# Two expert rankings, unscaled token rows and a folded tail in a four-layer routed kernel

## The chip, the cores and the metric

The kernel runs on one core of one Trainium2 chip. The metric is the device time of one execution in microseconds. TensorE (PE in the profile), VectorE (DVE), ScalarE (ACT), GpSimd (POOL) and SyncE (SP) each run an instruction stream of their own and meet only at semaphores; SP issues most DMAs, POOL the indirect ones.

## The reference

The input is 16 sequences of 256 tokens of width 128, in float32. Four residual layers follow one another, each on the layer norm of its input. Cut to what is computed:

```python
# 1: "attention": softmax over the keys is contracted away from v, so it sums to one
att = softmax(einsum('blhd,bmhd->blmh', q, k) * scale, axis=2)
opt = einsum('blmh,blhd->blhd', att, v).reshape(b, l, d)
x = x + opt @ w_out.T + b_out            # i.e. (v @ w_out.T + b_out)
# 2 and 4: mixture of 8 experts, the best 2 for each token
gate_logits = xn @ gate_w
top_vals, top_idx = top_k(gate_logits, 2)
top_w = softmax(top_vals)
h = relu(einsum('td,edf->etf', xn, w1))          # d 128, f 512
x = x + einsum('etd,te->td', einsum('etf,efd->etd', h, w2), combine)
# 3: selective scan over the 256 steps, 16 states
delta = softplus((u @ W_x[:, :64]) @ W_dt + b_dt)
x = x + (scan(u, delta, A, B, C) + u * D) @ W_out + b_out
```

The two expert layers have the same weights `gate_w`, `w1` and `w2`.

## The kernel before

The 4096 tokens are worked in 8 blocks of 512 (`TB`). A block stays in on-chip memory as `x` (128 tokens in the partitions, 4 chunks, 128 wide). The attention layer is a matrix product with weights multiplied together beforehand (`wat`), and gives the logits of the first expert layer as well. The two expert layers are `k = 1` and `k = 2` in the code; from here on "layer 1" and "layer 2" mean these two. Each works through sets of blocks: `FIRST = ([0], [1], [2, 3], [4, 5], [6, 7])` and `SECOND = ([0, 1], [2, 3], [4, 5], [6], [7])`.

For each set, `route` chooses two experts for each token, counts tokens with products of 0/1 matrices (`both`, `before`, `onesb`), and so gives each token a place among an expert's slots. `choose` computes the shares of the two experts. For set [0] of layer 1 the rows go to their slots by products with 0/1 matrices (`spot`, `dealt`: `ramp` is compared with the place). For all other sets each row of 128 values is scaled and shifted by the share and the layer norm (`row`, on ACT or DVE) and scattered by GpSimd into a table in device memory (`slots`, `scatter` at L880, one indirect DMA for 128 tokens). `experts` then fetches the slots of one expert after another (`xs`), transposes them (`xsT`), multiplies with `w1` (into `ps_b` or `ps_B`), takes the relu (`h`), multiplies with `w2` (into `ps_y`), transposes back (`yT`, `yr`) and stores the result (`ys`). `collect` gathers each token's two rows (`yy`, L892, eight indirect DMAs for a block) and adds them to `x`. Since the share is positive, scaling the row ahead of the relu is the same as scaling the result.

A slot table is a list of (rows, columns) for each expert: `SLOTS` gives 8 slots of, say, 108 x 3 = 324. In layer 2 the experts are ranked once by their token counts (`ranking`, `RANKED = (2,)`), so that the largest slot goes to the fullest expert, and the weights are loaded again in that order: `load_experts` reads each rank's expert number from `which` into a register of SP (L934) and issues the loads of `w1` and `w2` (L935, L940). If a count exceeds a slot (`beyond`), the whole computation is done again by a general path at the end.

After each layer-1 set, `arrive` collects, takes the layer norm (`statistics`, `rstd_of`) and runs `mixer`, the selective scan of the set's blocks: logarithms and exponentials on ACT, scans and products on DVE, products with 0/1 selections on PE (`pieces`, `sel`). Its end multiplies the scan's result with `W_out`, and the input `u` with `wsd_s` = D times `W_out`. After each layer-2 set, `finish` collects, transposes and stores the result (`out_T`).

Nothing is issued as it is written down. Every operation becomes a job of a planner (`plan.job`, all recorded at L772), some with several engines to choose from (`either`). The planner starts jobs in the order of a list of ranks found beforehand (`ORDER`, packed text) and its own costs, and writes out each engine's program from the result. Where it foresees PE idle for 0.5 us or more, it inserts products of a block of zeros (`blank`, L1705), one for every 0.26 us. Buffers (`xT`, `row`, `yy`, `u`, `th` and others) have fixed numbers of copies.

Of the kernel before, what the change touches and what calls it, by code (L numbers as in the profile page):

```python
# [11 lines left out]
BF16 = mybir.dt.bfloat16  # L12
# [7 lines left out]
P = 128  # L20
L = 256
# [11 lines left out]
    {  # L33
        "first": ((88, 2),) * 8,
        1: ((84, 2),) * 8,
        2: ((108, 3),) * 8,
    },
    {
        "first": ((126, 3), (112, 3), (108, 3), (98, 3), (96, 3), (88, 3), (126, 2), (117, 2)),
        1: ((98, 2), (91, 2), (88, 2), (80, 2), (84, 2), (75, 2), (70, 2), (128, 1)),  # L40
        2: ((126, 3), (117, 3), (110, 3), (104, 3), (108, 3), (96, 3), (90, 3), (126, 2)),
    },
)
RANKED = (2,)
UNIT = 2
JOIN = 2

COLD = 5.0
# [14 lines left out]
    "c-qZZ2V4_p|G(!F2uWCBZ^GVNMD}nMWhmmpRjsY4t)oufI_lQiswi$nt>RvFf>K)%!~%*UB1=HoJFEa1cmE`Jxw{}(`+wi}^LZ0U"  # L63
    "a?kVJZ+?H@-|v>G_^I*=>c6NNCEAl^pxer^W>rkfI9&R;>iv%8rd7`B9lu02joA1NUDGqgsne+5m*>sC|3s_)i)v%K>WE364%f`z"
    "G%9VWd>|BeK0IC08FfuyS$#TV!ssUsJvZ9pw@tBaV2TlOKM(^Ype&9CWvPXsXYyKG+Pu%zXlZI1Sm&A}IY4CALbDer*&iR4gwV&l"
    "%_}jzc_s5zX!X3PvIWf#4x)X!&c}M*s#~aW*_FM4<>R>>-Ss7LRsE&oXUE3!i@n2)%YK;$2Ux%Q=KJd&AzO97EXmqll<=(G$|n86"
    "dYcDRExkEyN=&Uj^@^>Aca=O|2u`0WZ*KkZPp*nx>bjin<VsZC<o=9uRhFUFl+z=MPhNm~zw4pXzFM^_s$-IHUykn8ElEaxc^26-"
    "@4I$-U9_@v4^`W~w0Z1KeP?YmwJLUVr{|Jk*2t*vvi=>escnr%S2%5T@YvyUd1cK_&1T~j6D^|8^}R6ZVc4@5r`2UVu#9lkK^d>j"
    "<5raWMYj1fEzYZOy26KDMUnzv7Ki#3$Js3MGeWdkH_RQX!$+g^SGwX*L0g)m*&ht^hr`B{m+-Z+MtiQ=%kQlyO?ID9`_|x>g>x4a"
    "7{0aWT9KvwE7Mny<Gx<_BC^rwXq|G-%~+*L?XOC-N_X*TlWs>d*t>6dr4MgmZ>V5Cdl#UwvuaJIa7A;6SkO9NyAy2)R#I*_c4irG"  # L70
    "f$}i1aA)c7s#VilXwygk=1!Yh4K5@zA4WBp!hdS2*QXZDe|&PBD<YV-*P?Y!iDl#0qE3S>ix*QK?M<<E=x(XAp(VMh1?XG@R;LUe"
    "^+r5mvX*|O{~BSeh+)#r_1}t5_Zhr&a6Vyi`WybF4oh}yO!N4+5htCOsU-6w+usb|b1Ki@BBPCK;{T?1ty+gYBRIVexWd-=;yaSJ"
    "&s)c$pQk1Mu(kK>{gXydj2^f9i*!A>vkJ$Aory7?vCXs9d*QbqY<=vPD_5viZHRw+xyi_Maei$clW%G}<<Bhkhz`r&MH-;Cg^e&a"
    "U3gYoEtvixd0S^(bWqX_ezZ?DQW4gCxKZW)U-sXiwFV<^9XWugj&I$OH!^<jINSI_Rp(0X8CAy1J2}<+XY8MsQOzx+FI`ck!)UF1"
# [12 lines left out]
    "W}lxb*X~)HAE-1pB;BQ^LG!O|{!7wateXuPjy1g47G;AAOE#v|-`IO4l;JX=Le)SmG4aUQQQ6kXA%1z9t<NK0dmq^jAGBJpuKxgd"
    "eXkawFZ5$JMr2mlKB{8c=h)_Zy$KD=PPGs%xvk#g-~MD_9aH;}d%czM@ozmdc5X7%n7k(1V&fu#xkh5jB_tPq;C45@tIXzkaGgr;"
    "`U-V}elJ1K5|2t9!%F4Ie79N)zMgFdqAF5lr;az799pBdl=r?p=s{9t<;`CXoASO{t7VrlBRG@0J_1I0K8Wt`_lI$swmu6BI^+PG"
    "R<t`R#ilQeDPFoWaTfD_W-45&V`fle={DiT+;e$tuyA_JGv2os@98-1FqqaFKEJbL>3+MFs}kA@zjoxM2@bBZ-Zv|~*-qnO412%B"  # L90
    "Hrl?39I;U2Nl)*kc{(>WG8$)ax|gm~8_)17zHBvazRBVuOO~Pjb<fxgT5}Y$rBU13yY<|T>gT@6y{t2fvzNc1KieD~H?c3yIG5%1"
    "EZC;L<sGZu9pMPV16%ccCfxd9<XECrYvkB!<h1ocr=`%<`N@intL=VX)*h7_ooi=p!&4c>U}btmTfv<omWIQ-a$8N>Cfiq*;mz*K"
    "X~Rn9R^2?n+niWz_x`eL{ozpO&1-+YWLh^$VDQqHpSVriI0n@^F|pk#E1}=9&or)NWV*op*e;vXrU5-JJxh-3Fk{-vL_ZWd-(`H2"
    "k@>2&TjXi*rq>P$e>>}7fV!t%UxR&U@8s&d;UV$g>F5|2Zpc2S=4zO^Jm5y+3zK*Htk~qyL5(?+wC+!_Zq6Cy`MkJ=^V`TyeWuXt"
    "&YapiOGBTs*#<0g<ztSzO#Mb4*Oi?TS!SZ4o^E#ZOhD4zQ=R+|Ixbw%HSS}*_Wf~Z>nrHuK4p{B+fH~UE>nKqtaR_P_PR4V=)GIP"
    "!Ikr-C#gjoJ>T&4m`N)*+szxBUi?zstQE)^-*auA<Lrx}7Gn-|ZG9f9D$<H~iw)(J4uc)c&AfL9uaDPpx~_b%G&X4U1Ad5jy|0kt"
    "-q%m7eTec@?E3E4PPX$n(aU-rFg1Mb6W;3N3jQ<IiG33%{1O-0xc2P#Mc2LUH4C!)1d=i2$+S8jbn2MmrUfI44!n=6D`;&|bw8)y"
    "MfYYF)pRR$)vNK;YU^v8rn%{zpSh*DMQ>#O<%u3}gHdkWyZcHxnY}jZ*J4i7EpLtfqkWEhOIbWuuiJ~hV{K6Q^&if?00DY0hVOmz"
    "w(r2s*FMAf{wuvbzY9&%5hrHsZXcB!Frs-!vd?v~)$Q@#yhiOE3(d+F)HQFI-@S##Q8iU@>%DG>IK7Hv8*S0w$rzhkaXC6o)ji8s"
    "`!Bs^j7RVnPN~uUeqGnob@xW?s`toU?B})Hci%{(+x}N#%V$Pprx$y2*!ij>)2t(qr7We8OpgM4w#&%LI@|8^R%NLE{xFwj+K}6m"  # L100
    "b#UGJVz!Frr07J=%-<$(E^!5ZPiC$>cICE-+9D&MvC_q=&c?IIp#PomyfstNq`8xn_PPi{-i^Qb^B4icKWSfnWuEpshKGMXO-KBa"
    "=BoRm!22z7$df~xYih~RD4J0_uHf#=@y4}b4=0M=y}F&4Z()!27mYJDP#W|4r2qBc5k6+ZsmEp;lr-B_g}@On;%JxdtZy7=+QdGx"
    "yla*QO+TGe7qCPrt6tNs!1LsF+YX1c?FNBPU%_hnsIm6g1-Z(n%9a$4aLcXI(=D#wS?k^4&KOZ*`&&}y{2h1Nf(s*Ou)a7J-V;=5"
    "`P4q4-{LJlR5<M0=6>%|UzTqL+sN`e7sJ_KZg8@&@au7ONDB*z{gWFQUT1pQv}Vx+x9Hik#V7Rl+Z)hgxUIJA$4R$lKR?^2v3_#!"
    ">)PnR%R2jnzwLTu3Uu|kbtp<>T=OyQvM-&@w&$T@l}_3ZQ*NSLbH51^?E9;{t@f*o)tW*1N!vbj^|Lw3#=Yep4jt^mESpJxfC&!u"
    "_j<e<oHm85F<l%mC!pg^x#5;03HD#!nfc|W!Yv&~&3er&Hy#Y)c(sHwV#d^Ud=anS!QbqV|0JrT#@hFbW6e=28?RYgY;T}n^*esh"
    "+f#V-iGLybGSv_*tJ;;?#RTx?(>iSLS`GI|w-ybT=8a5-_S(Yg$bBX;2j0eVis|qA3g-E?KhJwV&Eu78T5)&z_y-)N`nxw$=*&I4"
    "nhaG+6Gw5t#PeFdh8BM?nN!+Kv}|TAVpYGdJksWFbWPdEPrax`*`nI_smPJjoW9V~)4$rh{Hwd?rzM>5KH{xeU~?{qv)X@bwaNGe"
    ")x-IJX?GXCn)i~Eud^+i|FF}2fgg*J(jGL=RLf9Ds3%lLgmgZP3Rit!p{KueP0iNqr)s^1@ATAXG1~3xEHC=8+jSqsm<GQY-k>pQ"
    ")26Pj?OzImt0t%IsMxt?=i!-Gh6e~9#%wsV?(#{Io<pJE>XcJn%Ns6MP24iQF89_rCD#Uf-P`BFQ~M6Jc2~515XG41nN2a6)1;bE"  # L110
    "m9@~*SLdZJ(|1(cZ01i#E9Vq@<!E+PUq1frrHS4?A+2}9m|xC1VIK0-!PJeR+T5nr?um*uelVfaw1czLr>d(b&f%Z*r3db5o>pvD"
    "`NQjpr{~RJ>@8@V<dHV^YS9#ylOs6LK3xClqaeM6-{Nw4$gz<rc6I;iujBWg&9<GqpiZA&YIlNb<X8M){?VWfCRNMIbh&NiE1&N1"
    "Z)j9s@Gvl`Y>8Xtz7RCT=GVN5u`IzgtLDSyJ$X|nn{9KuYVNy<-8-VKtT=$@bYzTU#`UzY*>5iKJ9gj9*!RX?q?ymqFZ`{jH=#dF"
    "LMgBGR>#`RU)1{GUJx_TxW`#X6lteYa@u-UM?{JPr%!4B&Uj^?lyyz|di?iqoTuHYJHFy^@6W$RU;VLQX5R=0?W@+@lIqBsIAigQ"
    "Lod6vLU(*~aevVHb7lFXY*M;Z+Wy7P8RO4teqXL1baF~l;@4^Gy48K7qFi-Wq+Lk(v!+AUC%4M)+MJagRk=b$>!C|sL46-2d7&r@"
    "N#BU%r}R?#DY-%+WdQ<7_W-_(;(PcvgdId>OEMv{f5~ZpP}U&qn>;Vyk*^VQrB?uvE0BExF(v`C60;V<h06_x#Q-}(SOXDiAqWAO"
    "9t7V8*xiz4L?(|^0O1NC=_ZPj#zOd8Vvgi?>>L7PTYz*yeh9w<m28P&6v5&Li-{nRj#K=Wg&eaDk;WbZ0QZDADR&JL(l8l77D!Y?"
    "NAb8(WXevF@qoyPqY|qS5uL~+L}rNyvpi$cILWqvKyHiF8!S)=;i>EdN~RK5i-#WjM+k4QyJf<qP?2VtP)Ec=43nP7v?BNcdA!9i"
    "Ay}qI?hA~_)+Oh$$YFLtG!f|-EXJ~fJ1n~oA<F>Zctc1}@N)<}0Q#605Y=-CONJCE2&RMz4IBX2Zv>Uelct-fKnO<|0ScKsF{uKD"
    "U<|SdL_s~7X$1cvko^L<ZXhdYIXD4IDP7qT20f|oR7Su~hyel<<sl0m>8j*5sWmiduBAo-nh*jI!3oke2u5-KkmVX7s!RdhKujqk"  # L120
    "dDbCH3W!paMhSr+62An-3BjZS5e!jiMj}q6jNpYYtq*zB5itx=M9DxeF$l)xU_d5`2e(oL<EaD)iB;kNW-eZqhzxLeZ2K65<<fuY"
    "r6Mw9-?C*YM#*Y`Aju|4j2M6cW+_4tk|b3q?kh<-eKL2k6d?eY4)DCngd=!ip@0MoHCytE#JraJCriA{Ln$9(?gBC%5TsDtq}h;S"
    "_E0%a@Km9IC@48aQ9FSg8Hjuf_f%d5&`0!#P@^cvJ_5+nl@T^dFflY}^^z?TC8=L54Iv=mOzA|BtVCddP-t9YA3y+E=h!BtxrzZ{"
# [1652 lines left out]
```

## Time and profile before

| | us |
|---|---|
| median of 3 runs (lowest to highest) | 471.61 (468.14 to 472.38) |
| the profiled execution | 467.84 |
| its span, first to last instruction | 466.1 |
| PE busy, 2670 records | 447.0 |
| of these, products of `blank`, 232 records | 31.2 |
| DVE busy | 345.6 |
| POOL busy | 311.8 |
| ACT busy | 268.3 |
| data moved by DMA | 55.37 MB, mean 119 GB/s |

The span is what the profile divides into stages; the time of an execution is 1.7 us longer than the span here. A group in the profile is named by its line, engine, operation and the tiles that it writes and reads. Nearly all groups have line 772, because all operations are recorded there, so the tile names tell them apart.

### The profile page before, as it was taken

What the parts mean: (1) busy time and instruction counts of PE and PEld (TensorE: products, weight loads), DVE (VectorE), ACT (ScalarE), POOL (GpSimd) and SP (SyncE); (2) the same over time, 40 slices, a digit from 0 to 9 for tenths busy, and PEclk for the clock granted to TensorE, in tenths of its full rate; (3) what the DMA queues carried; (4) which work ended last, traced back from release to release, by engine and by line L of the source; (5) the groups of instructions that cost most, each with busy time, mean ns of one, the idle gap of its engine ahead of it and who ended that gap; (6) DMA issues with size and microseconds to landing.
All of it is one profiled execution on the core that took longest, in us unless ns stands there. A gap on an engine that the chain in (4) does not pass through costs nothing.

```text
span 466.1 us, 8797 instructions
## 1 busy us (share of the span) xinstructions
PE 447.0 (96%) x2670; PEld 355.8 (76%) x2670; DVE 345.6 (74%) x1229; ACT 268.3 (58%) x621; POOL 311.8 (67%) x482
## 2 busy tenths in 40 slices
PE   8999999999999999989997999989999999999994
PEld 6889998866766667665665777677678877999993
DVE  4799999778697878999999998996786931223420
ACT  2124443577576854995889496797735534343310
POOL 8188787777673761276866776836785477778662
PEclk9999999999999999999999899999999999999999
DMA  5974234632352423236644322144225333543251
GB/s 155 340 244 135 71 122 134 166 107 66 108 155 67 114 78 96 65 106 195 188 121 142 93 73 76 53 120 132 69 58 146 114 113 90 135 125 91 78 164 45
DMA packets 74917, 55.37 MB, mean 119 GB/s; under 512 B 8184, under 2 KB 66800, under 8 KB 74864
## 3 DMA queue, kind: packets, MB, share of 16 engines
q1 hardware_dynamic: 66640, 38.35, 28.5%
q0 software_dynamic: 7936, 16.27, 12.1%
q8 instruction: 23, 0.38, 0.4%
q14 instruction: 30, 0.25, 0.2%
q10 hardware_dynamic: 288, 0.13, 0.1%
HBM read 28.95 MB, written 25.77 MB: 117 GB/s over the span
## 4 chain that ended last, share of the span: by engine, by line
PE 72%; DVE 16%; ACT 4%; issue 3%; POOL 2%; DMA 1%; POOLq 0%; DVEq 0%; ACTq 0%
PE ps_b L772 25%; PE ps_y L772 24%; PE ps_B L772 21%; DVE x L772 3%; DVE ps_B L772 2%; DVE stats L772 2%; PE ps_y L1705 2%; POOL yy L892 2%; DVE w L772 1%; DMA yy<-ys,of 1%; DVE th L772 1%; ACT th L772 1%; DVE rt L772 1%; ACT decay L772 1%; DVE u L772 1%
## 5 line engine op out<-in xcount | busy, mean ns | idle before, releaser
L892 POOL DMA_INDIRECT yy<-ys,of x128 | 125.5, 980 | 64.4 <-issue 37.2
L880 POOL DMA_INDIRECT slots<-row,to x120 | 120.6, 1005 | 49.5 <-issue 19.4
L772 PE MATMUL ps_y<-h,w_s 128*128 128x324 f32 (+13 forms) x552 | 145.2, 382 | 0.0
L772 PE MATMUL ps_B<-xsT,w_s 128*128 128x324 f32 (+9 forms) x352 | 112.8, 442 | 0.8 <-DVE w L772 0.4
L772 PEld LDWEIGHTS ps_y<-h,w_s 128*128 128x128 f32 x552 | 90.4, 190 | 20.3 <-issue 1.3
L772 PEld LDWEIGHTS ps_B<-xsT,w_s 128*128 128x128 f32 x352 | 61.7, 191 | 23.8 <-issue 3.2
L772 ACT ACTIVATE h<-ps_B 128x648 f32<-128x648 f32 (+9 forms) x62 | 43.8, 707 | 33.5 <-PE ps_B L772 33.1
L772 PE MATMUL ps_b<-xsT,w_s 128*128 128x176 f32 (+9 forms) x288 | 54.8, 316 | 1.2 <-ACT yr L772 1.2
L772 PEld LDWEIGHTS ps_b<-xsT,w_s 128*128 128x128 f32 x288 | 44.1, 190 | 2.7 <-ACT yr L772 1.5
L772 ACT COPY yT<-ps_y 128x324 f32<-128x324 f32 (+14 forms) x52 | 18.8, 362 | 36.0 <-PE ps_y L772 35.2
L772 ACT ACTIVATE th<-later,lneps,ha_s 128x112 f32<-128x112 f32 (+13 forms) x85 | 39.1, 507 | 0.2 <-DVE th L772 0.2
L772 ACT ACTIVATE h<-ps_b 128x352 f32<-128x352 f32 (+9 forms) x47 | 22.3, 474 | 26.0 <-PE ps_b L772 24.1
L772 PE MATMUL ps_b<-ident,yT 128*108 128x128 f32 (+11 forms) x177 | 34.4, 274 | 0.7 <-ACT yr L772 0.7
L772 ACT COPY xsT<-ps_b 128x324 f32<-128x324 f32 (+15 forms) x52 | 19.1, 372 | 26.6 <-PE ps_b L772 25.3
L772 ACT ACTIVATE decay<-delta,nea 128x108 f32<-128x108 f32 (+13 forms) x85 | 31.7, 412 | 2.7 <-DVE delta L772 2.6
L1705 PE MATMUL ps_y<-blank,ones_d 128*128 128x128 f32 x232 | 31.2, 293 | 1.3 <-DVE blank L772 1.3
L772 DVE TENSOR_TENSOR_SCAN w<-decay,ps_B 128x360 f32<-128x360 f32 (+7 forms) x40 | 31.0, 802 | 1.3 <-ACT decay L772 0.5
L1705 PEld LDWEIGHTS ps_y<-blank,ones_d 128*128 128x128 f32 x232 | 30.0, 208 | 1.6 <-DVE blank L772 1.3
L772 ACT COPY yr<-ps_b 108x384 f32<-108x384 f32 (+13 forms) x50 | 21.3, 425 | 16.8 <-PE ps_b L772 16.8
L772 ACT ACTIVATE row<-x,mp,rp 128x128 f32<-128x128 f32 x63 | 28.1, 488 | 3.6 <-DVE rp L772 2.0
L772 PE MATMUL ps_b<-ident,xs 108*128 108x108 f32 (+13 forms) x186 | 29.7, 256 | 0.1
L772 DVE TENSOR_SCALAR h<-ps_B 128x648 f32<-128x648 f32 (+6 forms) x26 | 21.3, 819 | 11.1 <-PE ps_B L772 10.8
(207 smaller groups left out, 792.2 us busy)
## 6 DMA issues: line engine op xcount, KB each, us to landing
w_s<-in_w SPq DMA_DIRECT2D x32, 256.0 KB
xs<-slots SPq DMA_DIRECT2D x27, 162.0 KB
ys<-yr SPq DMA_DIRECT2D x27, 162.0 KB
slots<-blank SPq DMA_DIRECT2D x2, 1280.0 KB
xT<-in_xT SPq DMA_DIRECT2D x8, 256.0 KB
yy<-ys,of POOLq DMA_INDIRECT x128
out_T<-xnT SPq DMA_DIRECT2D x8, 256.0 KB
slots<-row,to POOLq DMA_INDIRECT x120
```

The lines of the kernel that those rows point to most:

```text
L772: return lambda: f(*[real(x) for x in a], **{n: real(x) for n, x in k.items()})
L880: inst = nc.gpsimd.indirect_dma_start(out=real(out), out_offset=bass.IndirectOffsetOnAxis(ap=real(rows), axis=0), in_=real(in_), in_offset ...
L892: nc.gpsimd.indirect_dma_start(out=real(out), out_offset=None, in_=real(in_), in_offset=bass.IndirectOffsetOnAxis(ap=real(rows), axis=0),)
L1705: nc.tensor.matmul(out=spare, lhsT=ones_d.real(), rhs=blank.real(), start=True, stop=True,)
```

## The change

- `SLOTS` gives each set a table of its own, and layer 1 is ranked too, from set [2, 3] on: `RANKED = ((1, 2), (2, 0))`. The weights are therefore loaded three times instead of twice.
- Scatters send the unscaled rows of `x`. `w1` is centred when first loaded, by a product with `centre` (the identity less 1/128), so that the mean needs no subtraction; the share times the reciprocal deviation is applied in `collect`, with four `scalar_tensor_tensor` instructions for each gathered tile in place of one add.
- The centred `w1` and `w2` are written back to device memory (`w1c`, `w2c`) in the layout of on-chip memory, in runs of 2 KB; later loads come from there, with the eight expert numbers loaded into registers of SP at once (`look`).
- A set's slots lie one after another in the table, no longer interleaved by expert.
- `mixer` scales `u` by 2 D, adds the scan's result to it, and needs one product with `wsh_s` = half of `W_out`, where it had two.
- For the last set, [7] of layer 2, the results of the last three experts (`LATE = 3`) are not stored and gathered: `marks` builds each token's share at its slot as a matrix, and `finish` adds `yr` times the marks into the output's bank.
- In the dealing of set [0], the shares are left out of the 0/1 matrices, and ACT may build them too (`Away`: an absolute value and a relu). The reciprocal deviation of block 0 is started by a `pow` on POOL.
- `ORDER` is another list, and some costs of the planner differ. The number of inserted `blank` products follows from these.

```diff
-RANKED = (2,)
+RANKED = ((1, 2), (2, 0))
 UNIT = 2
+LATE = 3
...
-                idle[i] = (start[i] - free) * (1.0 if start[i] > COLD else 0.5)
+                idle[i] = start[i] - free
...
-    def load_experts(k):
+    w1c, w2c = dram("w1c", [NE, P, FF]), dram("w2c", [NE, P, FF])
+
+    def load_experts(q):
         for r in range(NE):
...
+                pw = bank("B", P, FF)
+                matmul(pw, centre, into[0])
+                copy(into[0], pw)
+                move(w1c[r], into[0], 4 * P * FF, took=0.5, turn="centred")
+                move(
+                    w2c[r], into[1].rearrange("p c d -> p (c d)"), 4 * P * FF, took=0.5,
+                    turn="centred",
+                )
...
-            k = (hot[:, t], ramp.rearrange("p c k -> p (c k)"), at[:, t, e : e + 1], m[:, 0, t, e : e + 1],
-                 ALU.is_equal, ALU.mult)
-            either(("DVE", "tensor_scalar", k, {}), ("POOL", "tensor_scalar", k, {}))
+            k = (hot[:, t], count, at[:, t, e : e + 1], None, ALU.is_equal)
+            either(
+                ("DVE", "tensor_scalar", k, {}), ("POOL", "tensor_scalar", k, {}),
+                ("ACT", Away, (hot[:, t], count, at[:, t, e : e + 1], one_c), {}),
+            )
...
+    def marks(q, f):
+
+        lo = q.starts[q.late]
+        n = q.rows - lo
+        hot = []
+        for t in range(NTT):
...
+            for i, v in enumerate((hot[t], other)):
+                V.tensor_scalar(
+                    v, tail, f[:, i, t : t + 1], q.share[:, i, t : t + 1], ALU.is_equal, ALU.mult
+                )
+            V.tensor_tensor(hot[t], hot[t], other, ALU.add)
...
-                r = new("row", [P, NTT, P], bufs=ROW)
-                for t in range(NTT):
-                    w, m = (v[:, i, lo + t : lo + t + 1] for v in (rp, mp))
-                    either(
-                        ("ACT", "activation", (r[:, t, :], xs_[b][:, t, :], AF.Identity),
-                         dict(bias=m, scale=w)),
-                        ("DVE", "tensor_scalar", (r[:, t, :], xs_[b][:, t, :], w, m, ALU.mult,
-                                                  ALU.add), {}),
-                        turn="row" if t == 0 else None,
-                    )
                 for t in range(NTT):
                     scatter(
-                        q.slots, idx[:, i, lo + t : lo + t + 1], r[:, t, :], f"in{q.name}",
+                        q.slots, idx[:, i, lo + t : lo + t + 1], xs_[b][:, t, :], f"in{q.name}",
...
-            product(xs_[b], xs_[b], y, ALU.add)
+            for t in range(NTT):
+                V.scalar_tensor_tensor(
+                    xs_[b][:, t, :], y[:, t, :], q.share[:, i, lo + t : lo + t + 1],
+                    xs_[b][:, t, :], ALU.mult, ALU.add,
+                )
...
-            matmul(so, wsd_s, u[:, i], True, False, hold=[sos])
-            matmul(
-                so.rearrange("p (s l) -> p s l", l=L)[:, :, L - KM : L], wsh_s,
-                whole[:, NSEQ * i : NSEQ * i + NSEQ], False, True,
-            )
+            own = slice(NSEQ * i, NSEQ * i + NSEQ)
+            product(ends[:, own], ends[:, own], whole[:, own], ALU.add)
+            matmul(so, wsh_s, u[:, i], hold=[sos])
...
+                for r, yr in q.made.items():
+                    last = r == NE - 1
+                    if last:
+                        for t in range(NTT):
+                            matmul(pt[:, ts(t, P)], xs_[b][:, t], ident, False, False)
+                    for c in range(q.room[r][1]):
+                        end = last and c == q.room[r][1] - 1
+                        matmul(pt, yr[:, c], q.rowsT[r, c], first, end, hold=[o] if first else ())
+                        first = False
```

## The prediction

> **What bounds the kernel now.** I read the busy shares and the 40 slices first, then the chain that ended last, then the table by stretches, then single stretches of the timeline.
>
> ```profile
> span 466.1 us, 8797 instructions
> PE 447.0 (96%) x2670; PEld 355.8 (76%) x2670; DVE 345.6 (74%) x1229; ACT 268.3 (58%) x621; POOL 311.8 (67%) x482
> ...
> PE   8999999999999999989997999989999999999994
> ...
> PE 72%; DVE 16%; ACT 4%; issue 3%; POOL 2%; DMA 1%; POOLq 0%; DVEq 0%; ACTq 0%
> ```
>
> PE is busy 96% of the span, but a busy PE need not do useful work: 232 of its records (116 products; a float32 product leaves two records, a transpose one) are products of `blank`, which the kernel inserts wherever its planner foresees an idle PE. The table by stretches, for those alone and then for everything, shows where:
>
> ```profile
> 0.00:20.00 20.00, 7.45 (x46) 7.32 (x46) 0.17 (x1) 1.00 0.80 234
> ...
> 200.00:265.00 65.00, 8.89 (x60) 8.16 (x60) 0.00 (x0) 0.97 0.50 146
> ...
> 444.00:466.20 22.20, 12.83 (x112) 12.66 (x112) 0.00 (x0) 0.95 0.33 104
> ```
> ```profile
> 200.00:265.00 65.00, 59.92 (x311) 42.08 (x310) 62.98 (x135) 51.40 (x109) 47.43 (x56) 0.97 0.50 146
> ...
> 345.00:444.00 99.00, 99.00 (x651) 86.83 (x650) 44.24 (x161) 42.87 (x101) 69.39 (x79) 1.00 0.39 110
> ```
>
> (Columns: PE, PEld, then DVE, ACT, POOL in the second fence, granted clock, DMA share, GB/s.) So there are four regimes: a head of 26 us bound by latency, a long body bound by PE, inside it a stretch at 200 to 265 us where DVE works 62.98 of 65 us, and a tail of 22 us in which PE only idles on `blank`.
>
> What does a PE product cost? The timeline in the body gives it:
>
> ```profile
> 199.76 1.25 PE L772 MATMUL ps_y<-h,w_s 128*128 128x324 f32 x4
> 200.86 1.25 PE L772 MATMUL ps_B<-xsT,w_s 128*128 128x324 f32 x4
> 201.95 0.27 PE L772 MATMUL ps_b<-ident,yT 128*108 128x128 f32 x1
> ...
> 204.56 3.06 PE L1705 MATMUL ps_y<-blank,ones_d 128*128 128x128 f32 x26
> ```
>
> From start to start, two products of 324 columns take 1.10 us: 1.69 ns a column. A `blank` product takes 3.06/13 = 0.235 us. A transpose takes about 0.11. With these I priced every PE instruction of both programs, in their orders.
>
> **The change part by part.**
>
> *PE work in the body.* The slot sizes of the ten sets shrink by 1097 columns in all (919 in layer 1, where 24 slots of 324 become 24 of 244 to 324; 178 in layer 2). Each column passes 8 products: 1097 x 8 x 1.69 ns = 14.8 us, of which 14.4 is had (the products laid out by row are 128 wide whatever the slot). Narrower transposes: -2.3. Skip term: 8 products of 360 columns go, -4.9. Centring `w1`: 8 products of 512 columns, +6.9, six of them ahead of the first dealt product and two (1.7) in the body. Marks: 16 transposes (+1.4) and four products of 512 (0.87 each), three of them in the body (+2.6). Counted instruction by instruction between the first dealt product and the last product into `ps_y`, PE work falls from 379.0 to 363.9 us: **-15.0**. PE has no idle there that could swallow it, so all of it shortens the path. `blank` products in that stretch go from 32 to 28: **-0.9**. The orders thus allow for the same waits.
>
> *The tail.* Before, the last product into `ps_y` ends at 444.15; then come the store of the last expert, eight gathers, the add, four transposes, a copy and the store of the result:
>
> ```profile
> 444.15 1.47 PE L772 MATMUL ps_b<-ident,x 128*128 128x128 f32 x12
> ...
> 447.55 0.94 POOL L892 DMA_INDIRECT yy<-ys,of  x1 [1.90 <-DVE x L772]
> 448.80 0.94 POOL L892 DMA_INDIRECT yy<-ys,of  x1 [0.30 <-issue]
> ...
> 456.29 0.94 POOL L892 DMA_INDIRECT yy<-ys,of  x1 [0.30 <-issue]
> ...
> 459.00 0.69 DVE L772 TENSOR_TENSOR x<-x,yy 128x512 f32<-128x512 f32 x1 [9.02 <-DMA yy<-ys,of]
> ...
> 460.54 0.59 ACT L772 COPY xnT<-ps_b 128x512 f32<-128x512 f32 x1 [14.68 <-PE ps_b L772]
> ```
>
> That is 21.9 us. After, the gathers need only the first five experts. Call T the transposes of the fifth expert's `yT`; behind it PE still has 9.2 us of products. First gather at T + 3.3 (the 444.4 to 447.55 here, copy to gather, is 3.2), seven more steps of 1.25 (8.75), 2.7 to the landing (456.29 to 459.00), then a multiply-add 0.34, one product with `ident` 0.23, the last mark product 0.87 and two handovers 0.2, and from the copy to the end the same 5.55: T + 21.95. The last `ps_y` product ends at about T + 9.4, so the tail is 12.5: **-9.4**. Upper end -12, if the first gather starts 2.6 earlier; lower end 0, if POOL comes late from the gathers of set [6], which stand ahead of these in its queue: they may start some 12 us of PE work before T + 3.3 and take 9 x 1.25 = 11.3, just enough.
>
> *The head.* First dealt product:
>
> ```profile
> 21.31 5.82 POOL L772 TENSOR_SCALAR u<-ramp,spot,shares 128x176 f32<-128x176 f32 x6 [10.13 <-DVE shares L772]
> ...
> 25.89 1.43 PE L772 MATMUL ps_b<-u,row 128*128 128x176 f32 x8 [0.36 <-DVE stats L772]
> ```
>
> POOL makes the four `u` of an expert in four steps of 0.99 after waiting for the shares. After, the shares are not needed (0.85 less), and DVE (0.40), POOL (0.99) and ACT (two instructions, by its 128x128 and 128x56 rows 0.43 to 0.49 each) build side by side, which saves up to 3. Against it stand six centring products (5.2) that must wait for `w1` to land and sit in PE's order ahead of the routing, and `pow` on POOL, which this trace does not have: between a one-element memset (0.09) and a 512-wide `tensor_tensor` (1.28), taken 1.0 since it is far smaller than the latter but no fill. PE work ahead of the first dealt product goes from 7.05 to 13.2 with 28 to 23 `blank`: at worst 6.1 - 1.2 = +4.9 later, at best 6 earlier. I take **-3**, nearest the build rows, because PE waits more than 10 of these 26 us and the `w1` products use that.
>
> *DVE.* The 128 scale-and-add steps of 128 columns are new. Nearest row, same form from PSUM: 344 ns, 44.0 us in all. They replace 20 adds of 512 (14.1) and 12 on POOL; the 57 row scalings (353 ns, 20.1) go. The marks add 8 tag products and 4 adds near 0.57 (the `h` of 392 columns): 6.8. In all +16.6, the upper end; 0 is the lower, since ACT loses 63 row scalings and has 13.6 us free at 200 to 265. Only there is DVE the bound: 21 gathers bring 21 steps (7.2) for 3 adds and 3 scalings (3.5): **+3.7**. The scatters now read `x` directly and wait for no scaling.
>
> [...]
>
> *Weights.* The first load is unchanged; 4.2 MB are written back centred and read twice, 8.4 MB more in all, beside a mean of 119 GB/s. I cost it at nothing. The cover: set [1]'s first expert frees its slot near 67 us, set [2,3] starts at 89.7 and takes 4 us an expert, so the last pair is due near 117; the reload before ran from 206.1 to 246.5, 40 us, so 107 here: 10 to spare. The queue of SP no longer loads `which` eight times (0.55 each); its one load now stands early, ahead of set [1]'s fetches, and waits for the ranking of [2,3].
>
> *Clock.* Granted clock is 0.97 at 200 to 265 and 0.95 in the tail. [...]
>
> **Sum.** 466.1 - 15.0 - 0.9 - 9.4 - 3.0 + 3.7 = 441.5 of span. The profiled execution took 467.84, 1.7 more than its span: 443.2. The median of the runs is 471.61, 3.8 above the profiled one; carried over: **447**.
>
> **Rivals.**
> - *The waits shrink too*: in the body some 30 us are neither products nor `blank`; DVE, free of scalings at 20 to 60 us (38.76 of 40 busy), could give back 8, so 439. For it: scatters wait for less. Against: the number of `blank` in the body hardly falls. 0.14.
> - *POOL keeps the tail*: the gathers queue up and the tail stays 21.9: 456. For it: 248 indirect DMAs at 1.25 us are 310 us of POOL. 0.14.
> - *DVE becomes the bound throughout*: the whole +16.6 is on the path: 447 + 13 = 460. 0.08; half of it counts as no change.
> - *Slower: the reload for [2,3] is late.* Place: its eight loads in SP's in-order queue, between fetches and stores. From 50 us on, each microsecond of reload goes onto the path; at 75 us (4.2 MB at 56 GB/s, about half of what the reload before had) the gain is gone, and at 85 the time is 482. Against: 105 GB/s in the reload before, in shorter runs. 0.07.
> - *It does not do what it says*: a slot overflows and the general path runs as well, over 1000 us more. Counting the tokens on the reference's inputs, the tightest slot keeps 3 free: 0.01.
>
> **Chances.** Forecast as summed 0.56, its own range 440 to 455. Faster by over 1% 0.88, within 1% 0.04, slower 0.08; 1% is about what a measurement of this kernel tells from no change. Range 436 to 462.
>
> **What would show it.** PE total near 426 with 146 `blank` records; last product into `ps_y` near 429; eight last gathers 1.25 apart beginning within 7 us *before* it; the first `u` product near 23; DVE near 360 busy. I am wrong if PE waits on `w_s` loads near 90 to 120 us, if DVE stands at 65 of 65 over a longer middle stretch, or if the last gather starts over 6 us after the last `ps_y` product.

## The result and the profile after

The changed kernel takes 571.65 us (median of 4, 570.8 to 573.0) beside 470.31 for the kernel before: a ratio of 1.2158, interval 1.2089 to 1.2227. I had said 447 and 436 to 462. In the visits to the chip behind this section the kernel before itself took 633 to 651 us (medians), except in those of h1_noreload and of n3_round with n4_split, so runs are compared by their ratios within a visit alone. The profiled execution took 573.0 us, its span 571.3.

The page of the changed kernel: span, busy times, PE in 40 slices, the chain that ended last by engine and by line.

```profile
span 571.3 us, 8720 instructions
...
PE 460.3 (81%) x2608; PEld 366.6 (64%) x2608; DVE 356.0 (62%) x1296; ACT 255.8 (45%) x585; POOL 284.6 (50%) x535
...
PE   7899999895687987169972499988997697959595
...
PE 44%; DMA 31%; DVE 14%; issue 3%; ACT 3%; POOL 2%; SPq 1%; POOLq 0%; ACTq 0%; DVEq 0%
PE ps_y L785 16%; PE ps_b L785 15%; DMA xs<-slots 15%; PE ps_B L785 11%; DMA ys<-yr 9%; DMA yy<-ys,of 5%; DVE ps_B L785 2%; DVE x L785 2%; POOL yy L920 2%; DMA slots<-x,to 2%; DVE w L785 2%; DVE stats L785 1%; PE ps_y L1839 1%; DMA w_s<-w1c 1%; DVE th L785 1%
```

PE was a row of nines and now has holes from the tenth slice on. DMA, 1% of the chain before, is 31% of it, and nearly all of that is the fetch of an expert's rows (`xs<-slots`), their store (`ys<-yr`) and what hangs on it. The reloaded weights (`w_s<-w1c`) are 1%. The waits of the same kernel (us in total, times, longest):

```profile
POOL yy L920 <- DMA ys<-yr: 81.7, 6, 28.3
DVE x L785 <- DMA yy<-ys,of: 65.9, 23, 17.8
PE ps_b L785 <- DMA xs<-slots: 45.7, 13, 7.7
```

And the table by stretches (PE, PEld, DVE, ACT, POOL, clock, DMA share, GB/s), the stretch in which I had feared DVE, and the end:

```profile
200.00:265.00 65.00, 42.09 (x208) 28.78 (x208) 38.62 (x102) 31.95 (x66) 19.80 (x23) 0.82 0.16 50
...
500.00:571.00 71.00, 50.55 (x323) 45.57 (x321) 19.19 (x57) 15.41 (x42) 30.29 (x32) 0.86 0.27 76
```

Nothing is busy there: PE 42 of 65 us, DVE 39, and the 16 DMA engines 16%. A mean over 16 engines can hide that one of them is full. The timeline of SP's queue in that stretch points to it:

```profile
212.35 2.37 SPq L785 DMA_DIRECT2D ys<-yr  x1
214.82 2.95 SPq L785 DMA_DIRECT2D xs<-slots  x1
217.87 0.93 SPq L785 DMA_DIRECT2D ys<-yr  x1
218.90 5.72 SPq L785 DMA_DIRECT2D xs<-slots  x2
224.67 2.85 SPq L785 DMA_DIRECT2D ys<-yr  x1
227.61 4.85 SPq L785 DMA_DIRECT2D xs<-slots  x1
232.51 6.12 SPq L785 DMA_DIRECT2D slots<-blank  x1
```

The mere issue of one fetch or store (second column) takes up to 4.9 us here; one took 0.93. By their sizes these transfers have 94, 95 and 89 rows.

**Theories.** Theory 1: a transfer of K rows is dealt to as many DMA engines as the largest divisor of K up to 16, and the new slots have bad divisors. So far this is an assumption; e4_alone below tests it (103 rows land after 8.4 us, 104 after 2.5). By it, of the 149 fetches and stores after, 29 have a prime number of rows (one engine) and 32 would have two engines; of the 152 before, none had fewer than 11 (88 rows). Theory 2: the written-back and reloaded weights hold SP's queue, my own slower rival. Theory 3: the new written order is bad by itself.

### The profile page after: what moved, and what is told of

Same layout as the page of the kernel before. It is cut to its first block, busy times and chain, and to the rows that moved or that the text cites. A ratio compares the mean times of both kernels' runs of the same rounds, so it can differ in the third digit from the quotient of the medians.

```text
span 571.3 us, 8720 instructions
## 1 busy us (share of the span) xinstructions
PE 460.3 (81%) x2608; PEld 366.6 (64%) x2608; DVE 356.0 (62%) x1296; ACT 255.8 (45%) x585; POOL 284.6 (50%) x535
## 4 chain that ended last, share of the span: by engine, by line
PE 44%; DMA 31%; DVE 14%; issue 3%; ACT 3%; POOL 2%; SPq 1%; POOLq 0%; ACTq 0%; DVEq 0%
PE ps_y L785 16%; PE ps_b L785 15%; DMA xs<-slots 15%; PE ps_B L785 11%; DMA ys<-yr 9%; DMA yy<-ys,of 5%; DVE ps_B L785 2%; DVE x L785 2%; POOL yy L920 2%; DMA slots<-x,to 2%; DVE w L785 2%; DVE stats L785 1%; PE ps_y L1839 1%; DMA w_s<-w1c 1%; DVE th L785 1%
## 5 line engine op out<-in xcount | busy, mean ns | idle before, releaser
L920 POOL DMA_INDIRECT yy<-ys,of x128 | 123.3, 963 | 174.9 <-DMA ys<-yr 81.7
L785 PE MATMUL ps_y<-h,w_s 128*128 128x176 f32 (+21 forms) x528 | 141.0, 391 | 23.7 <-DVE yT L785 23.6
L908 POOL DMA_INDIRECT slots<-x,to x120 | 118.1, 984 | 46.5 <-issue 25.4
L785 PEld LDWEIGHTS ps_y<-h,w_s 128*128 128x128 f32 x528 | 92.6, 202 | 40.5 <-DVE yT L785 24.0
L785 PE MATMUL ps_B<-xsT,w_s 128*128 128x282 f32 (+17 forms) x336 | 110.2, 447 | 1.1 <-DVE w L785 0.7
L785 DVE SCALAR_TENSOR_TENSOR x<-yy,share,x 128x128 f32<-128x128 f32 x128 | 43.1, 348 | 66.0 <-DMA yy<-ys,of 65.9
L785 PEld LDWEIGHTS ps_B<-xsT,w_s 128*128 128x128 f32 x336 | 62.1, 203 | 25.0 <-issue 6.1
L785 PE MATMUL ps_b<-ident,xs 94*128 94x94 f32 (+25 forms) x182 | 35.0, 278 | 47.1 <-DMA xs<-slots 45.7
L785 PE MATMUL ps_b<-xsT,w_s 128*128 128x176 f32 (+12 forms) x304 | 60.4, 325 | 3.1 <-DVE xsT L785 3.0
L785 PEld LDWEIGHTS ps_b<-ident,xs 94*128 94x128 f32 (+25 forms) x182 | 23.8, 155 | 55.2 <-issue 23.8
L785 ACT COPY xsT<-ps_b 128x176 f32<-128x176 f32 (+26 forms) x54 | 19.8, 366 | 86.9 <-PE ps_b L785 85.1
L785 ACT ACTIVATE h<-ps_B 128x564 f32<-128x564 f32 (+17 forms) x62 | 41.7, 673 | 37.3 <-PE ps_B L785 29.2
L785 PEld LDWEIGHTS ps_b<-xsT,w_s 128*128 128x128 f32 x304 | 48.7, 196 | 5.4 <-DVE xsT L785 3.3
L785 PE MATMUL ps_y<-w_s,h 128*122 128x128 f32 (+6 forms) x232 | 37.2, 304 | 4.5 <-DVE yr L785 4.5
L785 PEld LDWEIGHTS ps_y<-w_s,h 128*122 128x122 f32 (+6 forms) x232 | 33.9, 213 | 9.1 <-DVE yr L785 5.1
L785 ACT ACTIVATE th<-later,lneps,ha_s 128x112 f32<-128x112 f32 (+14 forms) x85 | 39.5, 507 | 0.0
L785 PE MATMUL ps_b<-ident,yT 128*88 128x128 f32 (+19 forms) x169 | 36.7, 293 | 1.8 <-DVE xsT L785 1.3
L785 ACT ACTIVATE h<-ps_b 128x352 f32<-128x352 f32 (+11 forms) x52 | 23.9, 460 | 30.6 <-PE ps_b L785 29.7
L785 ACT COPY yT<-ps_y 128x176 f32<-128x176 f32 (+20 forms) x43 | 15.4, 359 | 44.2 <-PE ps_y L785 40.6
L785 ACT ACTIVATE decay<-delta,nea 128x108 f32<-128x108 f32 (+14 forms) x85 | 32.2, 413 | 0.1
L785 DVE TENSOR_TENSOR_SCAN w<-decay,ps_B 128x360 f32<-128x360 f32 (+7 forms) x40 | 31.7, 805 | 0.8
L785 PEld LDWEIGHTS ps_b<-ident,yT 128*88 128x88 f32 (+19 forms) x169 | 22.9, 149 | 9.8 <-issue 2.3
```

The costliest lines, as they stand in the source:

```text
L785: return lambda: f(*[real(x) for x in a], **{n: real(x) for n, x in k.items()})
L908: inst = nc.gpsimd.indirect_dma_start(out=real(out), out_offset=bass.IndirectOffsetOnAxis(ap=real(rows), axis=0), in_=real(in_), in_offset ...
L920: nc.gpsimd.indirect_dma_start(out=real(out), out_offset=None, in_=real(in_), in_offset=bass.IndirectOffsetOnAxis(ap=real(rows), axis=0),)
```

## The experiments

### One transfer alone: e4_alone

```
+    for K in (128, 127, 112, 109, 108, 103, 98, 96, 94, 95, ...):
+        nc.sync.dma_start(out=t[0:K], in_=slot(0, K))     # K rows of 1536 bytes
+        nc.vector.tensor_copy(mark, t[0:80, 0, 0:8])      # waits for it
```

> Transfers alone, one after the other: K rows of 1536 bytes from HBM to SBUF for sixteen K, each waited for before the next; no layer is computed, the output is the input. Theory 1: issue to landing goes by the divisor and not by the size: 128, 112, 96 rows near 2 us; 108, 104, 98, 90 near 2.1; 95 (5 engines) near 2.7; 94 and 106 (2 engines) 4.5 to 5; 103, 109, 89, 127 (1 engine) 7 to 10 us, 127 longest. Two of 103 rows issued together take twice as long as one (the same engine); 103 rows cut into 96 and 7 near 2.5. The rivals have no reason for a difference between 103 and 104 rows: all within 2 to 2.5 us.

DVE's waits (two of each size: sum, times, longest):

```profile
DVE mark L58 <- DMA in127x<-in_w: 19.7, 2, 9.9
DVE mark L58 <- DMA in109x<-in_w: 17.8, 2, 8.9
DVE mark L58 <- DMA in103x<-in_w: 16.9, 2, 8.6
...
DVE mark L58 <- DMA in106x<-in_w: 10.8, 2, 5.4
...
DVE mark L58 <- DMA in94x<-in_w: 10.0, 2, 5.1
...
DVE mark L58 <- DMA in95x<-in_w: 6.6, 2, 3.4
...
DVE mark L58 <- DMA in104x<-in_w: 5.0, 2, 2.5
...
DVE mark L58 <- DMA in96x<-in_w: 4.5, 2, 2.3
```

103 rows land after 8.4 us, 104 after 2.5: one row *more* is 5.9 us faster. By the engines of theory 1: one 7.6 to 9.9 (89 to 127 rows, some 60 ns a row), two 5.0 to 5.4, three 3.8, five 3.3, eleven or more 2.2 to 2.5. The traces show the landings; the numbers of engines are theory 1's, but for 103 rows, counted below. An estimate by it, 2.0 us and 62 ns for each row that one engine carries (6.4 us for 103 rows, below), comes within 0.25 us of the means of all sixteen sizes. (The first transfer of 128 rows, issued right behind a store of 2 MB, took 6.9 and is left aside; the second took 2.5.) The timeline of two transfers of 103 rows issued together, and then of 103 cut into 96 and 7:

```profile
226.22 0.17 DVE L58 COPY mark<-pa 80x8 f32<-80x8 f32 x1 [8.29 <-DMA pa<-in_w]
232.65 0.17 DVE L58 COPY mark<-pb 80x8 f32<-80x8 f32 x1 [6.26 <-DMA pb<-in_w]
...
235.28 0.17 DVE L58 COPY mark<-cut 80x8 f32<-80x8 f32 x1 [2.26 <-DMA cut<-in_w]
```

The second lands 6.4 us behind the first. The queue's packets (count, MB, share of 16 engines' time), while those two are moved (218.76 to 232.10 us) and while one of 104 rows is (82.80 to 83.84), say why:

```profile
q1 hardware_dynamic: 208, 0.32, 6.3%
...
q1 hardware_dynamic: 117, 0.16, 52.8%
```

Two transfers of 103 rows together use one sixteenth of the engines' time: *one* engine at a time works and the others idle. Cut, 103 rows take 2.26 us. Stores are no better; a load, a store and a load back, one after the other, take 6.1 us with 96 rows and 24.7 with 103:

```profile
173.87 0.17 DVE L58 COPY mark<-back 80x8 f32<-80x8 f32 x1 [6.13 <-DMA back<-room]
...
199.04 0.17 DVE L58 COPY mark<-back 80x8 f32<-80x8 f32 x1 [24.72 <-DMA back<-room]
```

Theory 1 holds for a transfer alone, to within 0.6 us of what was expected.

### Other rows in the kernel: e1_round, e3_before106, and why they tell little

e1_round rounds the rows of all sets, two of them so:

```
-        ((106, 3), (103, 3), (98, 3), (97, 3), (95, 3), (94, 3), (94, 3), (89, 3)),
+        ((108, 3), (104, 3), (98, 3), (98, 3), (96, 3), (96, 3), (96, 3), (90, 3)),
```

e3_before106 is the kernel before with

```
-        2: ((108, 3),) * 8,
+        2: ((106, 3),) * 8,
```

> The changed kernel with its slot rows alone rounded to numbers with a large divisor of at most 16 (94 to 96, 103 to 104, 109 to 110, 107 to 108, 127 to 128 and so on): the same jobs, the same written order, 4 to 17 rows more or fewer in a set. Theory 1 (a transfer of K rows is dealt to as many DMA engines as the largest divisor of K up to 16, so 103 or 97 rows go through one engine): the loss goes, 437 to 460 us, near my old 447; the idle time of PE behind xs<-slots falls from 45.7 to under 5 us and that of POOL behind ys<-yr from 81.7 to under 15. Theory 2 (the written-back and reloaded weights hold SP's queue): these are untouched, 555 to 575 us. Theory 3 (the new written order, or the lower clock that it brings, is bad by itself): untouched too, 555 to 575 us.

> The kernel before with 106 rows in place of 108 in the 24 two-block expert slots of the first layer and nothing else (48 columns fewer in each set of eight experts). Theory 1: 106 has no divisor between 2 and 53, so 48 transfers go through 2 engines in place of 12, each about 53 x 65 ns = 3.4 us in place of 0.6: 485 to 540 us against 470. Theories 2 and 3: none of the change is in it, 463 to 471 us.

Measured: 1.1179 (1.1117 to 1.1242) of before for e1_round, 1.0744 (1.0711 to 1.0777) for e3_before106. Neither is a clean test: the planner replays its ranks with each job's price, other rows change the prices, and the replay gives another schedule. e1_round's page has 668 `blank` records where the changed kernel has 146. The size had been coupled to the whole schedule. From here on, in runs with other rows, the schedule is written out job by job (order, engine, buffer, `blank`; the code is shortened):

```
-        end, start, way, buffer = self.made = self.forward(*self.ranks())
+        order, way, buffer, blank = unpack(FROZEN)      # as planned for the original rows
```

### Rows, cuts and a control: f1_round, f3_before106, e2_split, e2b_split, g1_after, g2_round

f1_round is e1_round's rows and f3_before106 is e3_before106's, each with its kernel's own schedule written out. g2_round is f1_round again, g1_after the changed kernel. e2_split and e2b_split keep the rows, and with them the planner's schedule, and cut each transfer (shortened):

```
-                move(x, q.part(q.slots, r), 4 * N * P, took=0.55, turn="fetch")
+                halves(x, q.part(q.slots, r), 4 * N * P, took=0.55, turn="fetch")
...
+            for lo, hi in [(0, K // 16 * 16), (K // 16 * 16, K)]:     # in halves, the empty one left out
+                nc.sync.dma_start(out=real(out[lo:hi]), in_=real(in_[lo:hi]))
```

> The changed kernel with its slot rows as they are, each xs fetch and each ys store issued as two transfers, the first of the largest multiple of 16 rows, the second of the rest. Some 70 DMA issues of SP more, all else equal. Theory 1: most of the loss goes (the first part lands on 16 engines in about 0.6 us, the rest is at most 15 packets); 445 to 480 us, the additional issues costing something. Theories 2 and 3: 565 to 590 us, since SP's queue only has more to issue.

> The rounded slot rows of e1_round again, now with the changed kernel's schedule written out job by job (order, engine, buffer and the 97 filling products as they were), because the planner, given other sizes, had made another schedule: 668 filling products on record in e1_round in place of 146. So the rows are now the only thing that differs from the changed kernel. Theory 1 (one engine for a prime number of rows): 437 to 462 us beside a before of about 470; no PE wait on xs<-slots above 1 us. Theory 2 (the reload) and theory 3 (the order): 555 to 575 us.

> e2_split again, beside a kernel before that should now be near 470 us and not 650: the visit of the first four runs slowed every long kernel. Rows as in the changed kernel, each xs fetch and ys store cut into a multiple of 16 rows and the rest. Theory 1: 445 to 480 us (ratio 0.95 to 1.02). Theories 2 and 3: 565 to 590 us (ratio 1.2 to 1.25).

> The kernel before with its own schedule written out job by job, and 106 rows for 108 in the 24 two-block slots of the first layer. By the transfers alone (e4_alone) a fetch or store of 106 rows takes 5.4 us where one of 108 takes 2.45, so each of the 24 experts starts and ends some 3 us later, and two of them share the two engines for 2 x 3.6 us of packets. Theory 1: 480 to 530 us. Theories 2 and 3: 462 to 471 us (the columns fewer are worth 24 x 6 x 8 x 1.69 ns = 1.9 us).

> The changed kernel itself, as a control: in the two visits so far the kernel before took 646 to 650 us in place of 470, with pauses of 5 to 20 us in which all engines but POOL stood still together, so numbers there can be compared only within a visit. If this visit is undisturbed: 571 us beside 470. If it is disturbed as well: theory 1 has the changed kernel clearly above f1_round (650), at 690 to 760, because it keeps the one-engine transfers; theories 2 and 3 have it at 650, equal to f1_round, since the rows would not matter.

> f1_round again, beside the control. Theory 1: 0.76 to 0.82 of the control's time if the visit is undisturbed (437 to 462 us), 0.85 to 0.94 of it if disturbed. Theories 2 and 3: 0.98 to 1.01 of the control in either case.

Measured, as parts of the time before: g1_after 1.1008 (1.093 to 1.1086), f1_round 1.0037 (0.9977 to 1.0097), g2_round 1.015 (1.0072 to 1.0228), e2_split 1.0134 (1.0102 to 1.0166), e2b_split 1.0237 (1.0165 to 1.031), f3_before106 1.0561 (1.0473 to 1.0648). Beside the control of the same visit, rounded rows take 653.14/709.93 = 0.92; theory 1 had 0.85 to 0.94 and theories 2 and 3 had 0.98 to 1.01. And in the kernel before, 106 rows for 108 alone, with fewer columns, cost 5.6%. Theory 3 falls: f1_round has the changed kernel's order to the last job, 146 `blank` records included. The 0.6 us in the expectations of e2_split and e3_before106 and the 65 ns a row were my estimates: in e4_alone a row took 62 ns of one engine, but 108 rows landed after 2.45 us, and 103 rows cut in two after 2.26.

### Which side costs more: h3_fetch

Only the fetches are cut, the stores are whole.

```
-            halves(q.part(q.ys, r), yr, 4 * N * P, took=0.55, key=f"out{q.name}")
+            move(q.part(q.ys, r), yr, 4 * N * P, took=0.55, key=f"out{q.name}")
```

> As e2_split, but only the xs fetches are cut into a multiple of 16 rows and the rest; the ys stores keep their one transfer with the changed kernel's rows. It tells which side of the one-engine transfers costs more: PE waits on the fetches (xs<-slots, 45.7 us in the changed kernel), POOL's gathers on the stores (ys<-yr, 81.7 us), and DVE and with it the next block on the gathers. Theory 1: between the control and e2_split, 1.02 to 1.08 of the time before in a disturbed visit, 480 to 530 us in an undisturbed one; the wait of PE on xs<-slots under 5 us, that of POOL on ys<-yr still over 50. Theories 2 and 3: as the control, 1.10 (disturbed) or 571 us (undisturbed).

1.0691 (1.0487 to 1.0895), between the control's 1.1008 and e2b_split's 1.0237. Part of the loss hangs on each side. POOL's wait on the stores stayed over 50 us as expected (61.8), but the wait of PE on `xs<-slots` (25.4 us in the control) fell only to 12.7 us, not under 5. That the cut fetches still queue behind whole stores would explain it; no run shows it.

### The reload, and the times beside a kernel before of 470 us: h1_noreload, n1_round, n2_split, n3_round, n4_split

h1_noreload is f1_round with

```
-                    [("SP", 0.55, f)], [t], of, late=-4.0 * P * FF, turn="weights", after=[seen]
+                    [("SP", 0.55, (lambda: None) if q.k == 1 else f)], [t], of,
+                    late=-4.0 * P * FF, turn="weights", after=[seen],
```

n1_round and n3_round are f1_round, n2_split and n4_split are e2_split.

> f1_round (rounded rows, schedule written out) without the 16 reloads of w1c and w2c for the first layer's set [2,3]: SP's instructions for them are left out, so that set computes with the experts in the first set's order and its output values differ. 4.2 MB of transfers fewer. Theory 1 with my old term 'weights: nothing': the same as f1_round, 1.00 to 1.02 of the time before in a disturbed visit, 437 to 462 us in an undisturbed one. Theory 2 (the reload): clearly faster than f1_round, 0.92 to 0.97 in a disturbed visit.

> f1_round in an undisturbed visit (the kernel before is back at 470 us). Rounded rows, the changed kernel's schedule written out. Theory 1, my other terms right: 437 to 455 us. Theory 1 with another term of my sum wrong by some 15 us, as h1_noreload suggests: 460 to 470 us. If the reload matters (theory 2 as a second cause): above h1_noreload's 463 by more than 5 us. Theory 3: 560 to 575.

> e2_split in an undisturbed visit: the changed kernel's rows, each fetch and store in two transfers. Theory 1: within 12 us above n1_round (some 75 more issues of SP at 0.3 us, and two landings for one). Theories 2 and 3: 565 to 590 us.

> f1_round, hoped undisturbed. From h1_noreload (463.15 us, first dealt product at 30.0, last product into ps_y at 447.6): theory 1 with the reload worth nothing 461 to 467 us; with the reload a cause of its own over 470; theory 3 560 to 575.

> e2_split, hoped undisturbed. Theory 1: 463 to 480 us, a little above n3_round for some 75 additional issues of SP; theories 2 and 3: 565 to 590 us.

n1_round 1.0013 (0.9969 to 1.0057) and n2_split 1.0253 (1.0168 to 1.0338) repeat what was known. h1_noreload: 463.15 us, 0.9865 (0.9837 to 0.9893). n3_round: 465.23, 0.9888 (0.9858 to 0.9919). n4_split: 464.82, 0.9881 (0.9846 to 0.9916). So the changed kernel with nothing but its rows rounded, or its transfers cut, is some 1.1% *faster* than the kernel before. The reload for set [2, 3] is worth the difference of 0.9888 and 0.9865, some 1.1 us and inside the intervals: theory 2 falls. The page of n4_split and, of n3_round, its wait on the stores and three issues of SP's queue (L776 in n3_round is L785 of the changed kernel):

```profile
span 460.1 us, 8934 instructions
...
PE 430.5 (94%) x2608; PEld 344.4 (75%) x2608; DVE 355.5 (77%) x1296; ACT 254.4 (55%) x585; POOL 289.0 (63%) x535
```
```profile
POOL yy L911 <- DMA ys<-yr: 25.6, 5, 11.3
```
```profile
186.08 0.31 SPq L776 DMA_DIRECT2D xs<-slots  x1
186.48 0.37 SPq L776 DMA_DIRECT2D ys<-yr  x1
...
195.28 0.57 SPq L776 DMA_DIRECT2D slots<-blank  x1
```

POOL's wait on the stores fell from 81.7 to 25.6 (17.7 before), PE's on the fetches is gone from the list, and an issue takes 0.3 us. Over the whole span the 149 issues of fetches and stores sum to 50.1 us of SP in n3_round, none over 1.0, and to 141.8 in the changed kernel, 28 of them over 1.5 us and four at 6.6 to 7.0, one of these alone in its row:

```profile
143.39 6.96 SPq L785 DMA_DIRECT2D ys<-yr  x1
```

### What was left of my sum: p1_nocentre, p2_halfadd, p3_narrowadd

All three are f1_round with one edit: p1_nocentre

```
-                matmul(pw, centre, into[0])
-                copy(into[0], pw)
+                silent(matmul(pw, centre, into[0]))     # the jobs stay, nothing is issued
+                silent(copy(into[0], pw))
```

and p2_halfadd, with 0:16 in place of 0:64 in p3_narrowadd,

```
-                    xs_[b][:, t, :], y[:, t, :], q.share[:, i, lo + t : lo + t + 1],
-                    xs_[b][:, t, :], ALU.mult, ALU.add,
+                    xs_[b][:, t, 0:64], y[:, t, 0:64], q.share[:, i, lo + t : lo + t + 1],
+                    xs_[b][:, t, 0:64], ALU.mult, ALU.add,
```

> n3_round without the centring of w1: the eight pairs of products by centre and the eight copies back are left out, so w1 is used and written back uncentred and the output differs. If the centring products, which stand in PE's order between those of the routing, delay the head: first dealt product at 24 to 27 us in place of 30, time 459 to 462 beside n3_round's 465 (0.976 to 0.984 of before). Rival: the head waits on POOL's power and on DVE's chain, which stay: first dealt product still at 29 to 30, time 464 to 466 less the two products in the body (1.7 us).

> n3_round with the 128 scale-and-add steps at half width (64 of 128 columns; the other half of the expert results is left out, so the output differs). By the rows near them (348 ns at 128 columns, 0.18 us at 32) a step takes about 0.25 us, so DVE does some 12 us less, same waits and same order otherwise. If DVE is what PE waits for at 180 to 320 us: 457 to 462 us (0.972 to 0.984 of before), PE's idle time in the body down from 40 to 31 to 36 us. Rival: PE waits there for chains of latency, not for DVE's work: 463 to 466 us, the idle time still about 40.

> n3_round with the 128 scale-and-add steps 16 columns wide (112 of 128 columns of the expert results are left out, so the output differs). From 347 ns at 128 columns and 293 at 64 (0.84 ns a column) a step takes about 252 ns, so DVE does 12 us less, all else equal. If DVE's work is what PE waits for: 457 to 461 us, 0.972 to 0.981 of before where n3_round had 0.989, and PE's losses in the body down by 5 to 8 us. Rival, chains of latency: 463 to 466 us, 0.985 to 0.991.

p1_nocentre 1.0105 (1.0026 to 1.0185), its first dealt product at 30.3: no earlier than the 28.9 to 30.2 of the runs that centre. But it isn't a clean answer either. The stretches of 10 to 28 us, and six products of `wat` in them, of p1_nocentre and of n4_split:

```profile
10.00:28.00 18.00, 13.81 (x72) 11.72 (x70) 14.05 (x100) 1.28 (x6) 7.29 (x61) 0.72 1.07 337
...
19.14 1.81 PE L776 MATMUL ps_B<-wat,xT 128*128 128x144 f32 x6
```
```profile
10.00:28.00 18.00, 15.33 (x82) 10.76 (x80) 14.47 (x103) 3.88 (x11) 7.69 (x61) 0.91 1.07 331
...
20.03 0.90 PE L785 MATMUL ps_B<-wat,xT 128*128 128x144 f32 x6
```

Without the centring products PE was busy for 13.81 of the 18 us and was granted 0.72 of its clock; n4_split had 15.33 and 0.91, n3_round 14.50 and 0.91. The routing's products took longer there (six of `wat` 1.81 us for 0.90), which may have eaten what was won; what lowered the clock, no run shows. p2_halfadd 1.0178 (1.0062 to 1.0294) and p3_narrowadd 1.0265 (1.0215 to 1.0315) are not faster than the 1.0013 to 1.015 of the same kernel with whole steps, though DVE did 7 and 14 us less (36.0 and 29.2 for 43.0). That fits the rival, chains of latency, but with repeats of one kernel as far apart as 1.0013 and 1.015 the ratios don't show it.

## Why the prediction was wrong

**The step that failed** is the first: "The slot sizes of the ten sets shrink by 1097 columns in all". I multiplied those columns by 8 products and 1.69 ns and was right about PE, but the same numbers are the row counts of 149 transfers, and I priced none of them: the fetches and stores stand at nothing in the sum, without a reason. The "I cost it at nothing" of the weights was about other transfers. With e4_alone's landings an estimate of the missing term is 29 x (8.4 - 2.4) + 32 x (5.2 - 2.4) = 264 us of later landings, on the high side, since 17 of these 61 move narrower rows. What of it lay on the path is 571.3 - 463.6 = 107.7 us of span, taken with the rows rounded. None of the signs I named as proving me wrong would have caught it: PE hardly waits on `w_s`, DVE is not at 65 of 65, and the changed kernel's last gather starts 4.8 us after its last `ps_y` product, under the 6 that I named. I had given "slower" 0.08, nearly all of it for a late reload, which did not come.

**Term by term**, by n4_split, which has the changed kernel's own columns. PE's time is the sum of its records at the prices of the prediction, its loss what lies between their starts beyond that.

- *PE work in the body*: 383.3 to 369.0, -14.3 for -15.0 (the parts listed there add up to -15.9; the -15.0 was the count). `blank` -0.9 as forecast, 146 records. The work was right. "PE has no idle there that could swallow it, so all of it shortens the path" was not: the body got only 1.2 us shorter, because PE's loss grew by nearly as much (see *DVE*).
- *The tail*: last product into `ps_y` ends at 446.99, the end is 13.1 later, for 12.5; the last eight gathers begin 7.4 us before it. Right; POOL did not keep the tail.

```profile
439.63 0.95 POOL L931 DMA_INDIRECT yy<-ys,of  x1 [0.78 <-issue]
...
446.17 0.82 PE L785 MATMUL ps_y<-w_s,h 128*127 128x128 f32 x6
...
448.40 0.95 POOL L931 DMA_INDIRECT yy<-ys,of  x1 [0.30 <-issue]
```

- *The head*: first dealt product at 29.92 for 23 (28.93 in n3_round); +4.0 where I took -3, inside my bounds (-6 to +4.9) and at their other end. Two lines of the kernel before, then the timeline of n4_split:

```profile
17.73 0.18 DVE L772 TENSOR_REDUCE at<-oh 128x4 f32<-128x32 f32 x1
...
19.98 0.24 PE L772 MATMUL ps_b<-both,onesb 128*128 128x32 bf16 x4
```
```profile
19.98 0.17 DVE L785 TENSOR_REDUCE at<-oh 128x4 f32<-128x32 f32 x1
20.97 0.35 DVE L785 SCALAR_TENSOR_TENSOR x<-ps_B,rstd,x 128x128 f32<-128x128 f32 x1 [0.82 <-PE ps_B L785]
21.93 0.61 DVE L785 SCALAR_TENSOR_TENSOR x<-ps_B,rstd,x 128x128 f32<-128x128 f32 x2 [0.61 <-PE ps_B L785]
23.04 0.17 DVE L785 TENSOR_TENSOR oh<-rank,at 128x32 f32<-128x32 f32 x1
...
25.69 0.24 PE L785 MATMUL ps_b<-both,onesb 128*128 128x32 bf16 x4
27.39 0.44 ACT L858 ACTIVATE u<-ramp,spot 128x176 f32<-128x176 f32 x1 [2.12 <-DVE rt L785]
...
29.92 1.36 PE L785 MATMUL ps_b<-u,x 128*128 128x176 f32 x8
```

  From the first `u` to the first dealt product it is 2.5 us (4.6 before), so the side-by-side build saves 2.1 of the "up to 3". But the ranking product stands at 25.69, 5.7 later than the 19.98 before. Some 2.3 us of that are there already when DVE comes to `at<-oh` (19.98 for 17.73); then DVE, in order, holds the first block's ranking until 23.04 behind additions of the other block, which themselves wait for PE's `ps_B` (0.82 and 0.61). I looked at PE's queue there, not at DVE's. That this order is the cause is read from the timeline, not tested, and what makes the first 2.3 us stays open.
- *DVE*: a step is 348 ns for the 344 predicted, DVE busy 355.5 for 360. But PE's loss in the body is 41.5 us for 27.7 before, +13.8 where I took +3.7 (bounds 0 and 16.6). The stretches of n4_split:

```profile
200.00:265.00 65.00, 57.52 (x338) 42.01 (x337) 62.01 (x198) 48.25 (x104) 43.77 (x59) 1.00 0.45 146
265.00:345.00 80.00, 76.68 (x441) 57.15 (x439) 74.70 (x200) 53.82 (x118) 51.62 (x76) 0.98 0.26 81
```

  I priced one dense stretch; DVE is now nearly as full in the next one, 74.70 of 80 for 67.94 before. Whether its work or its order makes PE wait stays open (p2_halfadd, p3_narrowadd). ACT is a rival that I left out: in the chain that ended last it has 10% where it had 4, and DVE 19 for 16. The chain of n4_split:

```profile
PE 63%; DVE 19%; ACT 10%; DMA 3%; issue 3%; POOL 1%; SPq 0%; ACTq 0%; DVEq 0%; POOLq 0%
```

- *Weights*: nothing, and some 1.1 us measured, inside the intervals. Right.

So +4.0, -1.2 and -8.8 for head, body and tail make 466.1 into 460.1; I had 441.5. Without the transfers I would still have been 18.6 us low, in a time of 465 just outside my range.

## What to carry to other kernels

When a size changes, list everything that takes it: the columns of a product may be the rows of a transfer, and here a transfer's time went by the divisor of its rows and hardly by its bytes (8.4 us for 103 rows, 2.5 for 104). When no engine is busy and the mean DMA share is low, look at how long SP takes to issue and at the landing of single transfers. A kernel with a replayed schedule can't be tested by changing a size unless the schedule is held fixed.

## What the runs showed of the hardware

- In e4_alone, K rows of 1536 bytes landed in 2.2 to 2.5 us for 88, 90, 96, 98, 104, 108 and 112 rows, in 3.3 for 95, 3.8 for 87, 5.0 to 5.4 for 94 and 106, and in 7.6 to 9.9 for 89, 103, 109 and 127; two transfers of 103 rows in one queue ran one behind the other (6.4 us apart, 6.3% of 16 engines).
- Where such transfers crowded in the changed kernel, SP's issues slowed down too: from 0.3 to as much as 7.0 us, and `slots<-blank`, a transfer from 128 partitions behind them, took 6.12 us to issue instead of 0.57. A slow issue alone is no proof, though: another `slots<-blank`, at 22 us, takes over 4 us in n3_round as well. Why the issue waits, no run shows.
- Cutting each transfer in two nearly doubled the issues (149 to 287), and n4_split equals n3_round (0.9881 and 0.9888). It has 162 columns fewer, though, and where the kernel before took 634 us the cut was slower than the rounding, n2_split 1.0253 beside n1_round 1.0013, so a small price of the issues is not excluded.
- DVE's scale-and-add took 347, 293 and 241 ns at 128, 64 and 16 columns (n3_round, p2_halfadd, p3_narrowadd): an eighth of the width still cost 69%.
